# Attention with its exponentials' buffers placed ahead by how long each is needed, and a first unit that lends two steps

## The chip, the cores and the metric

The kernel runs on one core of one Trainium2 chip. The metric is the device time of one launch in microseconds (us), as the median of several runs. The core has five engines that run side by side, each through its own queue in order: TensorE (PE in the profile; PEld is its weight load), VectorE (DVE), ScalarE (ACT), GpSimd (POOL) and SyncE (SP, which here only issues transfers). They are tied together by semaphores.

## The reference

Two layers are computed on an input of 4 images with 256 channels of 48 x 48 pixels, all in float32. The first layer, cut to what matters here:

```python
x = relu(batch_norm(conv3x3(group_norm(x))))
qkv = einsum('oc,bchw->bohw', qkv_w, x) + qkv_b          # 8 heads of d = 32
attn = softmax(einsum('bhdn,bhdm->bhnm', q, k) * scale)  # N = 48 * 48 = 2304
out = einsum('bhem,bhnm->bhen', v, attn)
x = x + proj_w @ out + proj_b
```

The second layer makes per-pixel filters from a convolution, applies them at five dilations, mixes the six results with a 1 x 1 convolution, and normalises over the batch. The change is in the attention of the first layer alone.

## The kernel before

The four images are taken one after the other. For each, a stage that is bound by TensorE (convolution and the q, k, v products of this image, woven with the dynamic filters of the image before) is followed by an attention stage, which runs without the other. There are therefore four attention stages.

Attention of one image is cut into nine units. Units 0 to 7 are one group of four heads (of the two groups) with 512 queries; unit 8, the last, takes the 256 queries left over for both groups. Each unit walks over the 2304 keys in 18 steps of 128 keys (`NT`), so a stage has 162 steps. The order is written out by hand in the loop at the end of `attention`, as a software pipeline of one step:

- `scores` (step i): TensorE multiplies the keys with the queries, 4 heads, one into a PSUM bank of its own (`so`) and three into another tile (`se`). Then ScalarE takes two exponentials of it, L1339 for one head (128 x 512) and L1340 for three (128 x 1536), into an SBUF tile `p` of 128 x 4 x 512. In the kernel before, all `p` are tiles of one tag with four buffers, used in rotation: step i takes the place of step i - 4, and has to wait until whoever reads that one is done.
- `weigh` (step i - 1, after the scores of step i have been issued): TensorE multiplies `p` with the values into `num` (L1365), and VectorE adds `p` into `acc` (L1380), from which the softmax's denominator is made later. Step 0 has no add of its own: the add of step 1 takes `p` of steps 0 and 1 together, so the place of step 0 is held until then.

In some steps VectorE is spared three quarters of that add: in the steps of `LENT` = 2, 5, 8, 11, 14 of units 1 to 8 (the last unit leaves out 14), VectorE adds only the first head, and GpSimd issues a transfer that adds the three others of `p` into a tile `extra` by itself (L1384, an accumulating transfer; the first of a unit is a plain copy, L1382). Such a step is called lent. The place of a lent `p` is free only when its transfer has landed. Each transfer waits for the one before it, as all write `extra`. At the end of units 1 to 7, VectorE adds `extra` to `acc` (L1387, called the closing add here); the last unit adds it on TensorE. `extra` lies in the first 1536 columns of `ring`, a tile that in the other stages holds convolution weights.

At step 1 of a unit `close(u - 2)` makes the denominators of the unit two back on TensorE (`den`) and divides on VectorE. At the end of a unit ScalarE copies `num` to `ao` (L1390). At step 6 of some units (3, 5, 7, and 8) the attention of finished rows is projected on TensorE and added to the residual on VectorE (L1463, with statistics, L661), and ScalarE does a few pieces of the next image's normalisation (L2562).

Of the kernel before, what the change touches and what calls it, by code (L numbers as in the profile page):

```python
# [8 lines left out]
F32 = mybir.dt.float32  # L9
# [8 lines left out]
P = 128  # L18
# [7 lines left out]
NT = N // P  # L26
# [7 lines left out]
QC = 512  # L34
SAFE = 60.0
LENT = (2, 5, 8, 11, 14)
NEVER = float("inf")
LATE = (4, 3)
AHEAD = 2500.0
# [18 lines left out]
def conv_preact_kernel(  # L58
# [493 lines left out]
    with tc.tile_pool(name="w", bufs=1) as wpool, tc.tile_pool(  # L552
        name="act", bufs=1
# [750 lines left out]
        def attention(b, q, k_, vT, pools, spare, project, scratch, following):  # L1304


            ps_s, ps_a, work0 = pools
            ao = keep("h", f"ao_{b}")
            zeros = work0.tile([P, D], F32, tag="zeros", name=f"zeros_{b}", bufs=1)
            nc.gpsimd.memset(zeros, 0.0)  # L1310

            extra = scratch.rearrange("p (j n) -> p j n", j=3)
            scratch = work0.tile([P, QC], F32, tag="rt", name=f"rt_{b}", bufs=1)

            whole, rest = N // QC * QC, N % QC
            units = [[(g, q0, QC, 0)] for q0 in range(0, whole, QC) for g in range(NH)]
            units.append([(g, whole, rest, g * rest) for g in range(NH)])
            assert NH * rest == QC
            heads = [slice(j * D, (j + 1) * D) for j in range(4)]

            def three(name):
                return ps_s.tile([P, 3, 512], F32, tag="s", name=name)

            def scores(u, m):
                s1, s3 = ps_a.tile([P, 512], F32, tag="one", name=f"so_{b}_{u}_{m}"), three(f"se_{b}_{u}_{m}")
                for g, q0, n, at in units[u]:
                    for j, r in enumerate(heads):
                        dst = s3[:, j - 1] if j else s1  # L1330
                        nc.tensor.matmul(  # L1331
                            dst[:, at : at + n],
                            k_[r, g, m * P : (m + 1) * P],
                            q[r, g, q0 : q0 + n],
                            start=True,
                            stop=True,
                        )
                p = work0.tile([P, 4, QC], F32, tag="p", name=f"p_{b}_{u}_{m}", bufs=4)
                nc.scalar.activation(p[:, 0, :], s1, AF.Exp, scale=QS)  # L1339
                nc.scalar.activation(p[:, 1:, :], s3, AF.Exp, scale=QS)  # L1340
                return p

            state = {}
            last = len(units) - 1

            def weigh(u, m, p):
                if m == 0:
                    state[u] = dict(
                        num=ps_a.tile([P, 512], F32, tag="num", name=f"num_{b}_{u}"),
                        acc=work0.tile([P, 4, QC], F32, tag="acc", name=f"acc_{b}_{u}"),  # L1350
                    )
                st = state[u]
                several, end = len(units[u]) > 1, u == last
                if end and m >= NT - 2:
                    sums(u, p, m == NT - 2, m == NT - 1)
                    if m == NT - 2:
                        sums(u, st["acc"], False, False)
                        sums(u, extra, False, False, 1)
                if several and m == 0:

                    for j, r in enumerate(heads):
                        nc.tensor.matmul(st["num"][r, :], zeros, p[:, j, :], start=True, stop=False)
                for i, (g, q0, n, at) in enumerate(units[u]):
                    for j, r in enumerate(heads):
                        nc.tensor.matmul(  # L1365
                            st["num"][r, at : at + n],
                            vT[:, m, g * P + j * D : g * P + (j + 1) * D],
                            p[:, j, at : at + n],
                            start=(m == 0 and not several),
                            stop=(m == NT - 1 and i == len(units[u]) - 1),  # L1370
                        )
                if end and m >= NT - 2:
                    return
                if m == 0:
                    st["first"] = p
                else:
                    other = st["first"] if m == 1 else st["acc"]
                    lend = u > 0 and m in LENT[: len(LENT) - end]
                    js = slice(0, 1 if lend else 4)
                    nc.vector.tensor_tensor(st["acc"][:, js], other[:, js], p[:, js], ALU.add)  # L1380
                    if lend and m == LENT[0]:
                        nc.gpsimd.dma_start(out=extra, in_=p[:, 1:])  # L1382
                    elif lend:
                        nc.gpsimd.dma_start(out=extra, in_=p[:, 1:], accum_op=ALU.add)  # L1384
                if u and m == NT - 1 and not end:
                    rest = st["acc"][:, 1:]
                    nc.vector.tensor_tensor(rest, rest, extra, ALU.add)  # L1387
                if m == NT - 1 and not end:
                    g, q0, n, _ = units[u][0]
                    nc.scalar.copy(ao[:, g, q0 : q0 + n], st["num"])  # L1390

            def sums(u, rhs, start, stop, first=0):
                if start:
                    state[u]["den"] = three(f"den_{b}_{u}")[:, 0, :]
                for j, r in enumerate(heads[first:]):
                    nc.tensor.matmul(
                        state[u]["den"][r, :], ones, rhs[:, j, :], start=start, stop=stop
                    )

            def close(u):  # L1400

                if u < last:
                    sums(u, state[u]["acc"], True, True)
                else:
                    busy(ps_a.tile([P, 512], F32, tag="one", name="warm"), 5)
                st = state.pop(u)
                t = scratch
                nc.vector.transpose(t, st["den"])
                rc = work0.tile([P, QC // D], F32, tag="rc", name=f"rc_{b}_{u}")
                nc.vector.reciprocal(rc, t.rearrange("p (k d) -> p k d", d=D)[:, :, 0])  # L1410
                nc.vector.transpose(
                    t.rearrange("p (k d) -> p k d", d=D),
                    rc.unsqueeze(2).to_broadcast([P, QC // D, D]),
                )
                for g, q0, n, at in units[u]:
                    dst = ao[:, g, q0 : q0 + n]
                    src = dst if u < last else st["num"][:, at : at + n]
                    nc.vector.tensor_tensor(dst, src, t[:, at : at + n], ALU.mult)

            steps = [(u, m) for u in range(len(units)) for m in range(NT)]  # L1420
            prev = None
            chunk = 0
            for i, (u, m) in enumerate(steps):
                ps = scores(u, m)


                if m == 1 and u > 1:
                    close(u - 2)
                if prev is not None:
                    weigh(*steps[i - 1], prev)  # L1430
                prev = ps
                if m == 2 and u == last:
                    close(u - 1)
                if m == 6 and (u % NH == 1 or u == last):
                    while (chunk + 1) * CH <= units[u if u == last else u - 1][0][1]:
                        pp = three(f"pp_{b}_{chunk}")
                        pp = [pp[:, o] for o in range(NH)]
                        if spare:
                            spare.pop(0)()
                        project(chunk, ao, pp)  # L1440
                        chunk += 1
            assert not spare
            weigh(*steps[-1], prev)
            following[0]()
            close(last)
            following[1]()
            return ao, chunk
# [918 lines left out]
        for b in range(B + 1):  # L2366

            with tc.tile_pool(name=f"work1_{b}", bufs=2) as work1, tc.tile_pool(
                name=f"ps_c_{b}", bufs=2, space=PSUM
            ) as ps_c, tc.tile_pool(  # L2370
                name=f"ps_w_{b}", bufs=1 + (b == B), space=PSUM
            ) as ps_w, tc.tile_pool(
                name=f"ps_k_{b}", bufs=3 if b == B else 2, space=PSUM
            ) as ps_k, tc.tile_pool(
                name=f"ps_y_{b}", bufs=1, space=PSUM
# [194 lines left out]
            with tc.tile_pool(name=f"work0_{b}", bufs=2) as work0, tc.tile_pool(  # L2570
                name=f"ps_s_{b}", bufs=2, space=PSUM
# [3 lines left out]
                    lambda c, ao, pp, b=b, n=norm1: project(b, c, ao, pp, n), scratch, following,  # L2575
# [76 lines left out]
```

## Time and profile before

| | |
|---|---|
| runs shown | 2721.27, 2724.35, 2724.39 us; median 2724.35 us |
| profiled execution: time | 2722.09 us |
| profiled execution: span from first to last instruction | 2720.2 us |
| mean granted TensorE clock | 0.989 of full speed |
| attention stage of images 0 to 3 begins about | 152, 808, 1470, 2109 us |
| busy in 152 to 518 us (image 0): VectorE, ScalarE, GpSimd | 324.35, 323.22, 32.10 us of 366 |
| full add L1380 (128 x 2048), median | 2292 ns |
| add of a lent step (128 x 512), least | 682 ns |
| closing add L1387 (128 x 1536), 28 of them | 1757 ns |
| exponentials L1339 and L1340, mean | 599 and 1449 ns |
| transfers issued on GpSimd: L1382 (32), L1384 (124) | 555 and 849 ns to issue |

The durations are of one profiled execution, the runs are separate ones. In a row of the profile `acc<-acc,p` means that the instruction writes `acc` and reads `acc` and `p`; `se` and `so` are the scores, and `ring<-p` are the transfers of lent steps, since `extra` is a piece of `ring`. "Idle before" is the time for which the engine stood still ahead of an instruction, and the name after the arrow is what ended it. Where an instruction waited for several semaphores, the one that came last is named. TensorE's busy time is modelled from pipelined matmuls, so its share is not a measure of how much room it has.

### The profile page before, as it was taken

To read this page: it belongs to the slowest core of one execution; us is meant where nothing else is said; L and a number is where in the kernel's file an instruction comes from. 1 tells how busy PE (TensorE), PEld (TensorE's weight loads), DVE (VectorE), ACT (ScalarE), POOL (GpSimd) and SP (SyncE) were. 2 spreads that over 40 slices of the span, in tenths; PEclk is the share of its full clock that TensorE was granted. 3 is DMA by queue.
4 is the path that set the end of the run, shared out by engine and by line. 5 is a ranking of instruction groups with operands and counts; after the bars stand their busy time and mean duration, and the time that the engine had idled before them with its cause. 6 is when DMAs were issued, how large, how long until landed. Compare 5 with 4: busy or idle time off the path is not lost. (4 is left out here: it accounts for less than half of the span.)

```text
span 2720.2 us, 42536 instructions
## 1 busy us (share of the span) xinstructions
PE 2607.0 (96%) x16938; PEld 1102.1 (41%) x16938; DVE 2082.2 (77%) x2029; ACT 1806.3 (66%) x2287; POOL 809.3 (30%) x885
## 2 busy tenths in 40 slices
PE   6999999999999999999999999999989999999996
PEld 5632222555562222355555222245546222235554
DVE  7768888757739898857774988885775888885676
ACT  4479888734449898854445888884444888875344
POOL 5200100477520010067750000007775000100453
PEclk9999999999999999999999999999999999999998
DMA  4805445323252445423324354452324444432456
GB/s 174 223 13 105 108 98 110 90 60 108 65 104 58 99 95 108 99 74 87 94 63 84 76 105 99 94 111 75 84 73 120 107 100 99 99 88 72 121 165 219
DMA packets 136942, 273.67 MB, mean 101 GB/s; under 512 B 58024, under 2 KB 98384, under 8 KB 135712
## 3 DMA queue, kind: packets, MB, share of 16 engines
q0 software_dynamic: 26256, 137.71, 22.1%
q1 hardware_dynamic: 110480, 133.17, 18.3%
q8 instruction: 135, 2.21, 0.3%
q14 instruction: 71, 0.58, 0.1%
HBM read 112.12 MB, written 36.04 MB: 54 GB/s over the span
## 5 line engine op out<-in xcount | busy, mean ns | idle before, releaser
L1380 DVE TENSOR_TENSOR acc<-acc,p 128x2048 f32<-128x2048 f32 (+1 forms) x568 | 1052.0, 1852 | 121.0 <-ACT p L1340 71.6
L1340 ACT ACTIVATE p<-se 128x1536 f32<-128x1536 f32 x648 | 938.7, 1449 | 0.0
L1331 PE MATMUL so<-q,k 32*128 32x512 f32 (+1 forms) x1440 | 729.1, 594 | 18.5 <-ACT p L1339 15.9
L1331 PE MATMUL se<-q,k 32*128 32x512 f32 (+1 forms) x4320 | 737.8, 594 | 0.0
L1365 PE MATMUL num<-p,vT 128*32 128x512 f32 (+1 forms) x5760 | 711.9, 561 | 2.2 <-ACT ao L1390 2.2
L1339 ACT ACTIVATE p<-so 128x512 f32<-128x512 f32 x648 | 388.4, 599 | 195.2 <-PE se L1331 89.0
L1331 PEld LDWEIGHTS so<-q,k 32*128 32x128 f32 x1440 | 216.7, 183 | 535.6 <-ACT p L1339 492.0
L1834 POOL TENSOR_TENSOR near<-near,prod 128x384 f32<-128x384 f32 x352 | 353.3, 1037 | 255.3 <-DVE prod L1828 246.4
L1384 POOL DMA_DIRECT2D ring<-p x124 | 105.5, 851 | 776.4 <-ACT p L1340 481.4
L1365 PEld LDWEIGHTS num<-p,vT 128*32 128x32 f32 x5760 | 137.1, 108 | 480.2 <-issue 449.7
L1828 DVE TENSOR_TENSOR prod<-wb,pad 128x768 f32<-128x768 f32 x192 | 181.9, 953 | 84.6 <-ACT wb L1815 51.8
L1331 PEld LDWEIGHTS se<-q,k 32*128 32x128 f32 x4320 | 227.3, 183 | 5.1 <-ACT p L1340 4.1
L1815 ACT COPY wb<-ws 128x384 f32<-128x384 f32 x216 | 108.5, 506 | 166.0 <-DVE prod L1828 129.0
L1382 POOL DMA_DIRECT2D ring<-p x32 | 17.9, 559 | 632.2 <-ACT p L1340 485.1
L1992 PE MATMUL py<-far,wsc 128*128 128x384 f32 x512 | 169.9, 487 | 0.0
L1536 PE MATMUL pg<-pad,wcat 128*45 128x384 f32 x864 | 146.7, 490 | 8.5 <-ACT lg L1594 8.5
L1255 PE MATMUL pq<-hid,wqkv 128*128 128x384 f32 x384 | 133.1, 501 | 15.0 <-ACT hid L1125 12.8
L1504 ACT COPY far<-far 128x512 f32<-128x512 f32 x86 | 90.2, 1108 | 81.1 <-PE far L1762 77.8
L1992 PEld LDWEIGHTS py<-far,wsc 128*128 128x128 f32 x512 | 96.2, 190 | 66.0 <-issue 1.8
L1255 PEld LDWEIGHTS pq<-hid,wqkv 128*128 128x128 f32 x384 | 73.1, 194 | 69.2 <-ACT hid L1125 15.1
L1380 DVE TENSOR_TENSOR acc<-p,p 128x2048 f32<-128x2048 f32 x36 | 82.2, 2285 | 20.8 <-ACT p L1340 14.6
L1736 DVE COPY_PREDICATED amat<-along_y,bmat 128x768 f32<-128x768 uint32 x72 | 92.0, 1277 | 2.4
(334 smaller groups left out, 2865.1 us busy)
## 6 DMA issues: line engine op xcount, KB each, us to landing
ring<-p POOLq DMA_DIRECT2D x156, 768.0 KB, 5.7
ws<-w_d SPq DMA_DIRECT2D x216, 192.0 KB
ring<-u_d SPq DMA_DIRECT2D x36, 512.0 KB
pad<-in_x SPq DMA_DIRECT2D x14, 1152.0 KB
xst<-in_x POOLq DMA_DIRECT2D x36, 192.0 KB, 3.7
x_d<-pad SPq DMA_DIRECT2D x36, 192.0 KB
u_d<-pad SPq DMA_DIRECT2D x12, 512.0 KB
y_d<-y SPq DMA_DIRECT2D x13, 384.0 KB
```

Source lines behind the costliest of these rows:

```text
L1255: nc.tensor.matmul(pq[:, :CH], wqkv[:, i, s, g * P : (g + 1) * P], hid[:, i, cols], start=(i == 0), stop=(i == NH - 1),)
L1331: nc.tensor.matmul(dst[:, at : at + n], k_[r, g, m * P : (m + 1) * P], q[r, g, q0 : q0 + n], start=True, stop=True,)
L1339: nc.scalar.activation(p[:, 0, :], s1, AF.Exp, scale=QS)
L1340: nc.scalar.activation(p[:, 1:, :], s3, AF.Exp, scale=QS)
L1365: nc.tensor.matmul(st["num"][r, at : at + n], vT[:, m, g * P + j * D : g * P + (j + 1) * D], p[:, j, at : at + n], start=(m == 0 and not s ...
L1380: nc.vector.tensor_tensor(st["acc"][:, js], other[:, js], p[:, js], ALU.add)
L1384: nc.gpsimd.dma_start(out=extra, in_=p[:, 1:], accum_op=ALU.add)
L1536: nc.tensor.matmul(pg[64 * s : 64 * s + NG, :CH], wcat[:, ii, k, :], shifted(ii, cc, k // 3 - 1, k % 3 - 1), start=(i == 0 and k == 0), st ...
L1815: nc.scalar.copy(pw[:, :CH], fetched[c, k][0])
L1828: nc.vector.tensor_tensor(prod.rearrange("p h (r w) -> p h r w", w=WW), wb, src, ALU.mult)
L1834: nc.gpsimd.tensor_tensor(cat[:, h], cat[:, h], prod[:, h], ALU.add)
L1992: nc.tensor.matmul(py[c][:, o, :CH], wsc[:, n * NH + i, o * P : (o + 1) * P], rhs, start=(n == 0 and i == 0), stop=(n == order[-1] and i = ...
```

## The change

It has two parts. First, which of the four places a `p` gets is no longer a rotation but is worked out ahead for all 162 steps: each of four places has a due time; a step takes the place that is due first (the lowest number among equals), and sets its due time five steps on where the step is lent, three steps on otherwise. Each place becomes a tag of its own with one buffer. The engines still wait for the actual readers of the place; the due times only choose which place. Second, unit 0 lends too, in steps 9 and 14 (`FIRST`), and so does a closing add. A function `lends` now says which steps of a unit are lent; for units 1 to 8 these are the same as before.

```diff
+FIRST = (9, 14)
...
+            last = len(units) - 1
+            steps = [(u, m) for u in range(len(units)) for m in range(NT)]
+
+            def lends(u):
+                return FIRST if not u else LENT[:-1] if u == last else LENT
+
+            until, home = [0] * 4, {}
+            for i, (u, m) in enumerate(steps):
+                home[u, m] = until.index(min(until))
+                until[home[u, m]] = i + (5 if m in lends(u) else 3)
...
-                p = work0.tile([P, 4, QC], F32, tag="p", name=f"p_{b}_{u}_{m}", bufs=4)
+                p = work0.tile(
+                    [P, 4, QC], F32, tag=f"p{home[u, m]}", name=f"p_{b}_{u}_{m}", bufs=1
+                )
...
-                    lend = u > 0 and m in LENT[: len(LENT) - end]
+                    lend = m in lends(u)
                     js = slice(0, 1 if lend else 4)
                     nc.vector.tensor_tensor(st["acc"][:, js], other[:, js], p[:, js], ALU.add)
-                    if lend and m == LENT[0]:
+                    if lend and m == lends(u)[0]:
                         nc.gpsimd.dma_start(out=extra, in_=p[:, 1:])
                     elif lend:
                         nc.gpsimd.dma_start(out=extra, in_=p[:, 1:], accum_op=ALU.add)
-                if u and m == NT - 1 and not end:
+                if m == NT - 1 and not end:
                     rest = st["acc"][:, 1:]
                     nc.vector.tensor_tensor(rest, rest, extra, ALU.add)
```

More of the change, by code (lines that the diff above doesn't have):

```diff
@@ L1343, in attention @@
             state = {}
-            last = len(units) - 1
             def weigh(u, m, p):
@@ L1418, in close @@
                     nc.vector.tensor_tensor(dst, src, t[:, at : at + n], ALU.mult)
-            steps = [(u, m) for u in range(len(units)) for m in range(NT)]
             prev = None
```

## The prediction, made before the changed kernel was run

> **What bounds the kernel now.** I read the page first, then the row of waits of the first exponential's line, then the timelines of ScalarE, GpSimd and VectorE around a few waits.
>
> The page (busy us, share, count; for groups: busy, mean ns of one, idle time before it):
>
> ```profile
> PE 2607.0 (96%) x16938; PEld 1102.1 (41%) x16938; DVE 2082.2 (77%) x2029; ACT 1806.3 (66%) x2287; POOL 809.3 (30%) x885
> ...
> L1380 DVE TENSOR_TENSOR acc<-acc,p 128x2048 f32<-128x2048 f32 (+1 forms) x568 | 1052.0, 1852 | 121.0 <-ACT p L1340 71.6
> L1340 ACT ACTIVATE p<-se 128x1536 f32<-128x1536 f32 x648 | 938.7, 1449 | 0.0
> ...
> L1339 ACT ACTIVATE p<-so 128x512 f32<-128x512 f32 x648 | 388.4, 599 | 195.2 <-PE se L1331 89.0
> ```
>
> TensorE's 96% says little here, as matmuls overlap. What counts is the attention stage: four images, each 366 to 371 us, 162 steps of two exponentials. In undisturbed steps the starts of the first exponential lie 2.067 us apart and ScalarE has no gap at all, so ScalarE sets the pace there. Any idle time before L1339 then lengthens the kernel. What that idle time waited for (view of line L1339):
>
> ```profile
> its engine sat idle before it (us, times) until:
>   PE se L1331: 89.0, 163
>   PE so L1331: 25.1, 31
>   DMA ring<-p: 23.9, 25
>   DVE acc L1380: 10.9, 22
>   issue: 2.5, 1
>   PE num L1365: 1.2, 1
> ```
>
> The TensorE rows are mostly the projections (step 6 to 7 of some units) and the denominators (steps 1 to 3), which this change leaves alone. The next rows are the subject: a place of `p` still being read by the accumulating transfer or by VectorE. One such case, timelines of ScalarE and GpSimd (start, duration, idle before it):
>
> ```profile
> 219.82 0.60 ACT L1339 ACTIVATE p<-so 128x512 f32<-128x512 f32 x1
> 220.31 1.45 ACT L1340 ACTIVATE p<-se 128x1536 f32<-128x1536 f32 x1
> 222.27 0.60 ACT L1339 ACTIVATE p<-so 128x512 f32<-128x512 f32 x1 [0.51 <-DMA ring<-p]
> ...
> 226.41 0.60 ACT L1339 ACTIVATE p<-so 128x512 f32<-128x512 f32 x1 [0.37 <-PE se L1331]
> ```
> ```profile
> 209.63 0.86 POOL L1384 DMA_DIRECT2D ring<-p  x1 [5.43 <-ACT p L1340]
> 215.88 0.85 POOL L1384 DMA_DIRECT2D ring<-p  x1 [5.38 <-ACT p L1340]
> 222.70 0.85 POOL L1384 DMA_DIRECT2D ring<-p  x1 [5.97 <-DMA ring<-p]
> ```
>
> This is unit 1, step 15 of the first image. Its place was lent at step 11, the transfer went out at 215.88 and landed about 6.3 us later, and the exponential starts the moment it lands. The next transfer, at 222.70, waited for the same landing. The line view of L1384 gives the spread of landings:
>
> ```profile
> DMA to landing us min/median/max: 5.7/5.8/7.4
> ```
>
> With four places in rotation a lent place comes round three whole steps after its exponentials end: 3 x 2.067 = 6.2 us. Issue (0.3 us later) plus landing (5.7 or more) is 6.0 or more, so the rotation has 0.1 to 0.4 us to spare, and any landing over 5.9 makes ScalarE wait. Last, VectorE where unit 0 passes into unit 1:
>
> ```profile
> 187.35 9.48 DVE L1380 TENSOR_TENSOR acc<-acc,p 128x2048 f32<-128x2048 f32 x4
> 196.74 2.29 DVE L1380 TENSOR_TENSOR acc<-p,p 128x2048 f32<-128x2048 f32 x1
> 199.13 11.87 DVE L1380 TENSOR_TENSOR acc<-acc,p 128x512 f32<-128x512 f32 x7
> ```
>
> A full add takes 2.29 and follows the last by 2.39, against a step of 2.067, so unit 0, which lends nothing, falls 0.33 us further behind with each of its 17 adds, until the places run out: ScalarE's timeline shows waits of 0.46, 0.46 and 0.27 for VectorE from 194.52 on.
>
> **What the Trainium skill says.** "DMA: Bandwidth & Descriptors", section "Rules for kernel authors": an accumulating DMA must wait for an earlier one's semaphore before it touches the same bytes. The trace agrees: L1384 waited 266.1 us in 45 cases for the landing before it, so transfers form a chain. "Perfetto Trace Analysis", section "Optimization Strategy": repeated gaps on the engine that should be saturated can mean too few buffers. The row of 25 waits for `ring<-p` is that. "SBUF — State Buffer", section "Who interferes with whom", says a DMA never contends with a compute engine; the full add takes 2.28 to 2.29 us with and without a transfer in flight here, so I charge none.
>
> **The change part by part.**
>
> *Places by due time.* I followed the new rule by hand. In units 2 to 7 a lent place returns after six steps (after five for step 5), steps 0, 1, 7 and 17 keep four, and nine others (3, 4, 6, 9, 10, 12, 13, 15, 16) get three. Per image 3 such shortened places are in unit 0, 8 in unit 1, 9 in each of 2 to 7, 7 in unit 8: 72, or 288 in all.
>
> What it removes: from ScalarE's timeline I took every start of L1339 less the one before, less 2.067. Summed over units 1 to 8 and steps 8 to 17 and 0 (where lent places return, and the echo: a wait of TensorE's of +0.25 two steps later and -0.24 between), the excess is 5.6, 9.1, 10.1 and 7.4 us in the four images, 32.1 together. Not all goes. Units without a place wait still show 0.05, the last unit 0.24: 28 x 0.05 + 4 x 0.24 = 2.4. Some 1.6 at 1668 is a spot where TensorE itself ran slow (eight matmuls took 2.20 instead of 1.07). That leaves 28.1.
>
> Does a lent place then wait at five steps? It is free for 4 x 2.067 = 8.3 us. The slowest step-5 case of the trace was issued 0.3 after its exponentials and landed 7.3 later: 7.6. At six steps it is 10.3; the worst chain (image 2, unit 4: landings 6.03, 5.73, 7.08, 5.74, each next issue 0.53 after a landing) recomputed without ScalarE's pauses has its latest landing 7.9 after the exponentials. No wait; bounds 0 and 3 us.
>
> Do three steps suffice? The place is wanted 2 x 2.067 = 4.1 us after its exponentials. Step by step I compared the end of the add with the start of the exponential three steps on: spare time is 1.0 to 2.2 us in plain units and 0.67 at step 6 where a projection runs (its two updates and statistics stand before that add on VectorE). A wait that does bind shows 0.10 of that as signal time, so 0.57 is truly spare. I take 0; upper bound 5 us. Behind a waiting exponential would stand all of ScalarE, then TensorE's next scores.
>
> *Unit 0 lends steps 9 and 14.* Two adds go from 2.29 to 0.68, 1.61 less each; VectorE gains the closing add of `extra`, 1.76 as in row L1387. In unit 0 the add of step 10 ended 0.7 to 1.2 us after the exponential of step 13 began, those of 15 and 16 2.3 after theirs: with three-step places and no lending they would bind. With 1.6 off at step 10 it is 0.4 to 0.9 early, with 3.2 off 15 and 16 are 0.9 and 0.2 to 0.6 early: tight but free. Into unit 1 VectorE carries 3.2 - 1.86 (add and gap) = 1.3 us less lag than now, enough to end the waits there. Their size: steps 1 to 6 of unit 1 hold 4.5 us of excess over the four images; the copy of `ao` on ScalarE, which stays, costs 0.33 in the first of these steps, 1.3 in all. 3.2 goes, plus 0.2 in unit 0 itself. The transfer (0.53 and 0.85 us on an idle GpSimd) falls in a stretch with the DMA engines empty (share 0.00 at 170 to 190). The four closing adds, 7.0 us in all, are hidden behind the exponentials; uncovered, that would be the price. `extra` lies in the first half of `ring`; the block loaded there ahead of the stage goes into its last third, so nothing waits on it. Unit 1's first lend (step 2) must now follow unit 0's closing add; that ends about 6.2 us after step 17's exponentials, the lend is due at 6.7.
>
> Sum: 28.1 + 3.2 + 0.2 = 31.5 off the stage. What follows starts from its end, so all of it counts. The profiled execution took 2722.1 (span 2720.2); less 31.5 is 2690.6. The median of the runs lies 2.3 above that execution; between the two I say 2692. Late next: TensorE's projections and denominators, and ScalarE's own 2.067.
>
> **The rivals.**
>
> *Half of it returns as waits on the chain of transfers.* Landing plus reissue is 5.75 + 0.53 = 6.28 against a lending period of 6.20, so without ScalarE's pauses the chain slips by 0.08 a transfer, and by up to 1.5 at each crowded one. If two crowded ones often met in one unit, perhaps half of the 28 would remain: 2706. Against it: never more than two over 6.3 in one unit.
>
> *No difference.* The places were not the cause: for instance the granted clock (mean 0.989, and the slow spot at 1668) falls as TensorE's pauses vanish: 2722. 1% of clock in a stage that ScalarE paces costs little, which speaks against it.
>
> *Slower: the three-step places wait for VectorE.* One mechanism: the release of a place by its add reaches ScalarE later than the spare 0.67 to 2.2. It decides from about 1.5 us of extra delay; at 1.75 the 288 places would wait some 0.15 each on average, 43 us: 2735 (an estimate). For it: VectorE has only 0.7 to 1 us of idle per three steps of a lending unit. Against it: units with no pause at all exist in the trace (unit 3 of image 0) and keep those margins.
>
> **How the numbers follow.** Forecast 0.79 (own range 2686 to 2699), half 0.09, no difference 0.05, slower 0.07. The range runs from 2685 (a run-to-run spread of 3 and no residue) to 2706, up to the half. A difference under 0.2%, 5.4 us, cannot be told from none: faster 0.88, same 0.05, slower 0.07.
>
> **What would show it.** In the row of L1339, `DMA ring<-p` and `DVE acc` nearly gone, TensorE rows 89.0 and 25.1 smaller only by the echoes; the stage 358 to 363 us an image; transfers 156 to 164 at unchanged landing times; closing adds 28 to 32. A new sizeable `DVE acc` row with starts at steps 9 or 13 would show the three-step places wrong; lasting `DMA ring<-p` at step 10 the five-step ones.

## The result, and the profile after

The changed kernel takes 2690.34 us (median of 4 runs, 2688.22 to 2694.2) against 2722.81 us (2718.02 to 2724.39) for the kernel before in the same measurement. The ratio is 0.9878, with a 95% interval of 0.9864 to 0.9892: some 33 us less. The profiled execution has a span of 2687.6 us against 2720.2. Lines have moved by 10 or 11: the two exponentials are now L1350 and L1351, the add of `p` is L1390, the closing add L1397, the transfers L1392 (first of a unit) and L1394.

What the first exponential waited for, in the changed kernel (us, times):

```profile
its engine sat idle before it (us, times) until:
  PE se L1340: 62.7, 61
  PE so L1340: 25.1, 31
  issue: 3.2, 1
```

The rows for `ring<-p`, for VectorE's `acc` and for `num` are gone: no exponential of the 648 waits for its place any more. The row of `se` fell from 89.0 us in 163 cases to 62.7 in 61. Some 17 us of what fell away is the echo: a start that a place held up is followed by a small wait for TensorE two steps later. Another 7.2 us in 37 cases were place waits under TensorE's name. In the kernel before, those exponentials began 0.10 us after the landing of the transfer from their place, just as the 25 cases of the row `DMA ring<-p` did, and 7 of the 22 under VectorE's name as well. So landings held up more exponentials than that row names. `so` stayed at 25.1: mostly the denominators, which the change does not touch.

The transfers themselves did not become faster (line view of L1394; the second fence gives the landing times):

```profile
its engine sat idle before it (us, times) until:
  ACT p L1351: 545.2, 83
  DMA ring<-p: 140.8, 24
```
```profile
DMA to landing us min/median/max: 5.7/5.8/7.7
```

The row `DMA ring<-p` has 24 cases here and had 45 before, but this does not mean that fewer transfers wait for the one before: the landing is often hidden behind ScalarE's name. By the landing times, 75 of the 128 accumulating transfers start 0.53 or 0.54 us after the landing of the one before, and in the kernel before it was 70 of 124 (0.53 to 0.58 us). The transfers still form a chain, then, and land in 5.7 to 7.7 us (5.7 to 7.4 before); only no exponential waits for them any more. Where unit 0 passes into unit 1, VectorE's and ScalarE's timelines of the first image now read:

```profile
185.46 10.28 DVE L1390 TENSOR_TENSOR acc<-acc,p 128x2048 f32<-128x2048 f32 x5
195.77 1.76 DVE L1397 TENSOR_TENSOR acc<-acc,ring 128x1536 f32<-128x1536 f32 x1
197.45 2.29 DVE L1390 TENSOR_TENSOR acc<-p,p 128x2048 f32<-128x2048 f32 x1
```
```profile
194.04 0.63 ACT L1350 ACTIVATE p<-so 128x512 f32<-128x512 f32 x1
194.53 1.48 ACT L1351 ACTIVATE p<-se 128x1536 f32<-128x1536 f32 x1
196.38 0.60 ACT L1350 ACTIVATE p<-so 128x512 f32<-128x512 f32 x1 [0.36 <-PE se L1340]
196.87 1.45 ACT L1351 ACTIVATE p<-se 128x1536 f32<-128x1536 f32 x1
198.44 0.60 ACT L1350 ACTIVATE p<-so 128x512 f32<-128x512 f32 x1
```

The closing add at 195.77 is new work, and yet the add of steps 0 and 1 (197.45 to 199.74) ends before step 4's exponential wants the place of step 0 at 200.51. The waits of 0.46, 0.46 and 0.27 us for VectorE have given way to one of 0.36 for TensorE.

Where the 32.6 us of span came from, from the starts of the first exponential, four images summed. "Excess" is what the distance from one start to the next has over 2.067 us:

| us | before | after | less |
|---|---|---|---|
| the four attention stages | 1477.1 | 1442.7 | 34.4 |
| of it: excess at steps 8 to 17 and 0 of units 1 to 8 | 32.1 | 1.1 | 31.0 |
| of it: excess at steps 1 to 6 of unit 1 | 4.5 | 2.0 | 2.5 |
| of it: excess at steps 8 to 17 of unit 0 | 0.3 | 0.1 | 0.2 |
| of it: a wait for TensorE at step 2 of unit 0 of the last image | 1.8 | 1.1 | 0.7 |
| everything else | 1243.1 | 1244.9 | -1.8 |

The last row is made of +2.1 ahead of the first stage, +1.4, +0.1 and -1.9 between the stages, and nothing after the last. The first stage begins at 154.5 us in this execution, at 152.4 in that of before, and between 152.2 and 153.7 in those of the experiments, so executions differ by about this much. Two pieces of the gain in the stages are such differences too. The 0.7 us at the start of the last image, and 1.6 of the 31.0 us, come from short stretches in which TensorE ran at half its clock; they fell differently in the two executions (see the last section).

### The profile page after: what moved, and what is told of

It is laid out like the page before. It is cut to its first block, busy times and chain, and to the rows that moved or that the text cites. A ratio compares the mean times of both kernels' runs of the same rounds, so it can differ in the third digit from the quotient of the medians.

```text
span 2687.6 us, 42540 instructions
## 1 busy us (share of the span) xinstructions
PE 2590.6 (96%) x16938; PEld 1095.0 (41%) x16938; DVE 2075.3 (77%) x2033; ACT 1808.6 (67%) x2287; POOL 814.3 (30%) x893
## 5 line engine op out<-in xcount | busy, mean ns | idle before, releaser
L1390 DVE TENSOR_TENSOR acc<-acc,p 128x2048 f32<-128x2048 f32 (+1 forms) x568 | 1039.3, 1830 | 96.2 <-ACT p L1351 44.5
L1351 ACT ACTIVATE p<-se 128x1536 f32<-128x1536 f32 x648 | 938.1, 1448 | 0.0
L1375 PE MATMUL num<-p,vT 128*32 128x512 f32 (+1 forms) x5760 | 699.5, 561 | 1.7 <-ACT ao L1400 1.7
L1350 ACT ACTIVATE p<-so 128x512 f32<-128x512 f32 x648 | 388.4, 599 | 158.9 <-PE se L1340 62.7
L1394 POOL DMA_DIRECT2D ring<-p x128 | 109.1, 852 | 809.3 <-ACT p L1351 545.2
L1375 PEld LDWEIGHTS num<-p,vT 128*32 128x32 f32 x5760 | 129.1, 108 | 475.0 <-issue 448.4
L1392 POOL DMA_DIRECT2D ring<-p x36 | 20.1, 558 | 560.6 <-ACT p L1351 272.1
L1390 DVE TENSOR_TENSOR acc<-p,p 128x2048 f32<-128x2048 f32 x36 | 82.3, 2285 | 21.5 <-ACT p L1351 14.6
```

What stands on the lines that cost most here:

```text
L1375: nc.tensor.matmul(st["num"][r, at : at + n], vT[:, m, g * P + j * D : g * P + (j + 1) * D], p[:, j, at : at + n], start=(m == 0 and not s ...
```

## The experiments

**The two parts, each alone, and a control.** The edits are to the changed kernel.

Places by due time only; unit 0 lends nothing:

```diff
-                return FIRST if not u else LENT[:-1] if u == last else LENT
+                return () if not u else LENT[:-1] if u == last else LENT
...
-                if m == NT - 1 and not end:
+                if u and m == NT - 1 and not end:
                     rest = st["acc"][:, 1:]
```

> The due-time places without the first unit's lending (unit 0 lends nothing and has no closing add; its places then rotate by four as before). Theory: the waits of the first exponential for lent places were the main cost, worth 28 us, so 2723 - 28 = about 2695 (2692 to 2699), with no 'DMA ring<-p' row before the first exponential and the 'DVE acc' row left only at the start of unit 1, about 1 to 1.3 us an image. Rival (the gain came mainly from VectorE's lag out of unit 0): about 2718.

2693.88 us, ratio 0.9901 (0.9887 to 0.9915). ScalarE's timeline at the same spot as above (image 0, from step 2 of unit 1):

```profile
194.36 0.60 ACT L1350 ACTIVATE p<-so 128x512 f32<-128x512 f32 x1 [0.46 <-DVE acc L1390]
194.85 1.45 ACT L1351 ACTIVATE p<-se 128x1536 f32<-128x1536 f32 x1
196.75 0.60 ACT L1350 ACTIVATE p<-so 128x512 f32<-128x512 f32 x1 [0.46 <-DVE acc L1390]
...
198.95 0.60 ACT L1350 ACTIVATE p<-so 128x512 f32<-128x512 f32 x1 [0.26 <-DVE acc L1390]
```

These are the waits of the kernel before, to 0.01 us. All place waits of the kernel are here: the row of waits before the first exponential has no `ring<-p` and this for VectorE:

```profile
  DVE acc L1390: 5.5, 14
```

So the due times removed the waits for transfers by themselves (the excess at steps 8 to 17 and 0 is 1.8 us, from 32.1), and left the lag out of unit 0 alone.

Unit 0 lends, but places rotate by four:

```diff
-                home[u, m] = until.index(min(until))
+                home[u, m] = i % 4
```

> Unit 0 lends steps 9 and 14, but all places rotate by four. Theory: only the start of unit 1 gains, 3.4 us: about 2719.5 (2717 to 2722); the 'DMA ring<-p' waits stay at 20 us or more. Rival (first unit is the main thing): 2700 or less.

2718.29 us, ratio 0.9981 (0.9974 to 0.9988). The excess at steps 1 to 6 of unit 1 is 2.0 us, as in the changed kernel; that at steps 8 to 17 and 0 is 29.5. The waits, from the same view:

```profile
  PE se L1340: 86.4, 158
  PE so L1340: 25.1, 31
  DMA ring<-p: 23.6, 26
  DVE acc L1390: 4.4, 6
```

The six left under `acc` stand at steps 12 and 15, where the places of lent steps come back, and not at the start of unit 1.

Four tags, but rotation and no lending in unit 0 (both edits above together):

> A control: four tags of one buffer each instead of one tag of four buffers, but places in rotation and no lending in unit 0. Theory: the tags do nothing by themselves, so 2723 within 4 us, and the same waits as before. Rival (the way the buffers are tagged changes which semaphores are waited for, and that is the gain): 2705 or less.

2724.42 us, ratio 1.0003 (0.9995 to 1.0011), with 25.9 us in 26 waits for `ring<-p`. The tags by themselves make no difference that can be measured. The parts add up: 0.9901 and 0.9981 multiply to 0.9882, beside 0.9878 for both.

**How much room the places have.** Lent places kept for seven steps, which squeezes others:

```diff
-                until[home[u, m]] = i + (5 if m in lends(u) else 3)
+                until[home[u, m]] = i + (7 if m in lends(u) else 3)
```

> The changed kernel with seven steps in place of five for lent places. Worked out by hand, steps 6 (units 1 to 8) and 9 (units 2 to 8) then get their place taken back after two steps. Theory: an add ends 2.3 us after the exponentials and later, the place is wanted at 2.2; so steps 6 and 9 wait 0.2 to 0.5 each in plain units, and where a projection runs (add of step 6 late) about 1.5 more. About 10 us an image, 40 in all: 2728 (2710 to 2740), with a 'DVE acc' row of 30 to 45 us. Rival (VectorE's adds do not decide over places, only landings do): 2690.

2721.97 us, ratio 0.9994 (0.9984 to 1.0004): the whole gain is gone, and no transfer is waited for. VectorE is waited for instead:

```profile
  PE se L1340: 75.5, 98
  DVE acc L1390: 38.5, 37
  PE so L1340: 25.1, 31
```

Timelines of VectorE and ScalarE in image 1, unit 3, where the place of step 6 is wanted at step 8:

```profile
947.09 0.56 DVE L662 BATCH_NORM_STATS2 stn<-pad 128x6 f32<-128x384 f32 x1
947.57 4.67 DVE L1390 TENSOR_TENSOR acc<-acc,p 128x2048 f32<-128x2048 f32 x2
```
```profile
946.38 0.60 ACT L1350 ACTIVATE p<-so 128x512 f32<-128x512 f32 x1 [1.12 <-PE se L1340]
946.87 1.44 ACT L1351 ACTIVATE p<-se 128x1536 f32<-128x1536 f32 x1
949.94 0.60 ACT L1350 ACTIVATE p<-so 128x512 f32<-128x512 f32 x1 [1.63 <-DVE acc L1390]
```

The first of the two adds is that of step 6. It starts when the projection's statistics are done and ends about 949.86, 2.29 us later; the exponential follows at 949.94. The size was right (30 to 45 us expected in that row), the list was not complete: besides step 8 (late by 0.22 to 0.5 in plain units, by 1.5 where a projection runs), step 3 of unit 1 was late by 1.3 to 1.5, since the place of step 0 there returned after three steps instead of four. One of the 37 waits stands in unit 0 of image 2. The places of step 9, also taken back after two steps, have no wait of their own: the add of step 9 ends 0.09 to 0.13 us before the exponential of step 11, as close as where a place does bind (0.09 to 0.10), after the echo had put off step 10 by 0.22 to 0.25. Three steps are thus too few for step 0, and two for step 6.

VectorE held up at step 6 where a projection runs, the spot whose room the prediction had read:

```diff
+                    if m == 6 and u in (3, 5, 7):
+                        for j in range(2):
+                            nc.vector.tensor_reduce(spent[:, j : j + 1], p[:, j], AX.X, ALU.max)
                     nc.vector.tensor_tensor(st["acc"][:, js], other[:, js], p[:, js], ALU.add)
```

> The changed kernel with two useless reductions of p (128 x 512 each, about 0.7 us) on VectorE ahead of the add of step 6 in units 3, 5 and 7 (12 places in all), to measure how much room the three-step places have where a projection runs. Theory: 0.57 us of room, so 1.4 - 0.57 = about 0.8 us of waiting at step 9 in each of the 12, 10 us in all: about 2700, the waits named 'DVE acc'. Rival (there is more room than that, since places are released earlier or VectorE catches up): 2690 to 2692 and no such row.

2695.99 us, ratio 0.9881 (0.9859 to 0.9902), which does not differ clearly from the changed kernel's 0.9878; the median is 4 us below the 2700 expected. The trace does tell them apart. Image 1, unit 3, VectorE and ScalarE:

```profile
938.93 1.26 DVE L1393 TENSOR_REDUCE spent<-p 128x1 f32<-128x512 f32 x2
940.11 5.47 DVE L1394 TENSOR_TENSOR acc<-acc,p 128x2048 f32<-128x2048 f32 x3
```
```profile
939.81 0.60 ACT L1351 ACTIVATE p<-so 128x512 f32<-128x512 f32 x1
940.30 1.44 ACT L1352 ACTIVATE p<-se 128x1536 f32<-128x1536 f32 x1
942.49 0.60 ACT L1351 ACTIVATE p<-so 128x512 f32<-128x512 f32 x1 [0.74 <-DVE acc L1394]
```

The reductions put the add off by 940.11 - 938.93 = 1.18 us, and the exponential of step 9 comes 942.49 - 939.81 - 2.067 = 0.61 us late. The room was therefore 1.18 - 0.61 = 0.57 us. There are 12 such waits (8.9 us of idle time in all, 7.3 us of excess), one for each of the 12 edited places and none elsewhere.

This is not the least room in the changed kernel. From the end of an add to the exponential that takes its place there are 0.66 to 0.69 us at step 6 with a projection, but 0.28 at step 16 of unit 0 in image 2 (0.64 to 0.79 in the other images), and 0.37 at step 0 of units 2 to 7, although that place keeps four steps.

**What holds the rest.** Denominators of a unit at step 3 of the next one, rather than at step 1 of the one after:

```diff
-                if m == 1 and u > 1:
-                    close(u - 2)
+                if m == 3 and u:
+                    close(u - 1)
...
-                if m == 2 and u == last:
-                    close(u - 1)
```

> The changed kernel, with the denominators of a unit made one unit later at step 3 instead of two units later at step 1. Asks what holds the 1.33 us that steps 1 to 3 of units 2 to 7 still lose. Theory: it is TensorE's work for the denominators plus ScalarE's copy of the outputs, two separate costs that stay wherever they stand: 2690 within 4 us, with the excess moved from steps 2 and 3 to 4 and 5. Rival: VectorE, which is late at that point (its add of step 1 ends only 0.4 us before its place is wanted), holds TensorE through the denominators' PSUM tile; then the move wins up to 0.5 us a unit, about 2676.

2695.47 us, ratio 0.9906 (0.9891 to 0.9921). ScalarE in image 1, unit 2, step 2 and then steps 4 and 5:

```profile
888.07 0.60 ACT L1350 ACTIVATE p<-so 128x512 f32<-128x512 f32 x1 [0.36 <-PE se L1340]
...
893.07 0.60 ACT L1350 ACTIVATE p<-so 128x512 f32<-128x512 f32 x1 [1.00 <-PE so L1340]
...
895.34 0.60 ACT L1350 ACTIVATE p<-so 128x512 f32<-128x512 f32 x1 [0.33 <-PE se L1340]
```

Less 2.067, the steps are late by 0.22 and 0.27 (steps 1 and 2: the copy of the outputs on ScalarE) and by 0.87 and 0.21 (steps 4 and 5: the denominators on TensorE). Apart they cost 1.57 us a unit; together, at steps 1 to 3 of the changed kernel, 1.33. The excess moved as the theory said, but the median lies 1.5 us above the expected range, and the four stages take 1453.1 us, 10.4 more than in the changed kernel. That the move costs 0.24 in each of units 2 to 7 was not expected; apparently part of one wait hides in the other when they meet, which was not tried further. Unit 1, which had no denominators to make before, now has 1.07 more in each image. A late VectorE is not what holds these steps: here it had itself been idle for 0.90 us before it took up the denominators, until TensorE had made them.

```profile
891.19 0.72 DVE L1418 STREAM_TRANSPOSE rt<-den 128x512 f32<-128x512 f32 x1 [0.90 <-PE den L1406]
```

An attempt at a faster version: the edit above, and the copy on VectorE ahead of the add of step 17:

```diff
+                    if m == NT - 1 and not end:
+                        g, q0, n, _ = units[u][0]
+                        nc.vector.tensor_copy(ao[:, g, q0 : q0 + n], st["num"])
                     other = st["first"] if m == 1 else st["acc"]
...
-                    nc.scalar.copy(ao[:, g, q0 : q0 + n], st["num"])
```

> An attempt at a faster version: the copy of the outputs at a unit's end goes from ScalarE to VectorE, ahead of the add of step 17, and the denominators are made at step 3 of the next unit (as in e7), so that VectorE has room at the unit's start. In e7 the copy costs 0.49 us at steps 1 and 2 of every unit after the first. Theory: that goes, less what TensorE waits for the later copy: 32 x 0.4 = 13 us below e7, about 2682 (2678 to 2688). Rival: TensorE's first value matmul of the next unit waits for the copy on the busier VectorE, and the gain is lost: 2695 or more.

2687.78 us, ratio 0.9858 (0.9841 to 0.9874). The interval overlaps that of the changed kernel, and the four stages sum to 1441.9 us against 1442.7: no clear gain over it. The copy's 0.49 us did go from steps 1 and 2. But in units 2, 4 and 6 step 7 now waits for VectorE, for the place of step 4, whose add comes after the denominators' work (image 1, unit 2):

```profile
897.83 0.60 ACT L1350 ACTIVATE p<-so 128x512 f32<-128x512 f32 x1 [0.38 <-DVE acc L1393]
```

With its echo that is 0.25 us a unit. Against the run with the later denominators alone the stages are 11.3 us shorter, near the 13 expected, so moving the copy did what it should; most of this only makes good the 10.4 us that the later denominators cost. The expected 2682 was 6 us too low.

## Why the prediction was right

The median is 2690.34 us where 2692 was forecast, and the forecast's mechanism holds at each step.

*ScalarE sets the pace, and its idle time ahead of the first exponential lengthens the kernel.* The stages lost 34.4 us and the span 32.6. The work between and after the stages did not give it back: the distances differ by -1.9 to +2.1 us, to either side. Of the 34.4, some 32 are owed to the change and 2.3 to where the half-clock stretches fell, beside a forecast of 31.5.

*Place waits for lent steps, put at 28.1 us.* They measured 31.0. The mechanism is shown by the two parts alone. One term was mis-sized: I had left 2.4 us as a residue of steps without a place wait, and 1.1 remain. The 0.05 a unit that I read as permanent fell to 0.02 or 0.03, the last unit's 0.24 to 0.10. The other difference is luck: I had taken off 1.6 for a spot where TensorE ran slow, and no such spot fell into these steps of the changed kernel's execution. The control with four tags, which has none there either, loses 2.40 us in that unit (image 2, unit 4) where the kernel before lost 3.92; but its excess over all units is 31.6, so the landings alone make executions differ by about 1 us.

*The start of unit 1, put at 3.2 us.* It measured 2.5. The copy of `ao` costs 0.22 and 0.27 us at two steps, and I had counted 0.33 at one. In the places-only kernel, which lacks this part, the excess at unit 1 is exactly that of the kernel before.

*Three steps suffice.* Yes, with the room that was read from the trace: 0.57 us where a projection runs, both as read and as measured by holding up the add. The tightest place, step 16 of unit 0, held with 0.28 us between add and exponential, where 0.2 to 0.6 had been worked out. The rival that ends slower was real as a mechanism and wrong in size: with one step less for a few places of each unit (lent places kept for seven steps) the whole gain is lost.

*No wait at five and six steps for lent places.* None came, but with less room than the prediction had it. I recomputed the worst chain to a landing 7.9 us after the exponentials. In the changed kernel, image 0, unit 6, GpSimd's and ScalarE's timelines show a later one:

```profile
403.23 0.85 POOL L1394 DMA_DIRECT2D ring<-p  x1 [6.09 <-ACT p L1351]
411.44 0.85 POOL L1394 DMA_DIRECT2D ring<-p  x1 [7.36 <-ACT p L1351]
417.74 0.85 POOL L1394 DMA_DIRECT2D ring<-p  x1 [5.44 <-ACT p L1351]
```
```profile
423.76 0.60 ACT L1350 ACTIVATE p<-so 128x512 f32<-128x512 f32 x1
424.25 1.45 ACT L1351 ACTIVATE p<-se 128x1536 f32<-128x1536 f32 x1
425.83 0.60 ACT L1350 ACTIVATE p<-so 128x512 f32<-128x512 f32 x1
```

The transfer at 403.23 took 7.7 us to land, so the next two went out late, the second (step 11) 2.4 us after its exponentials; it landed 6.38 us on, at 424.1, which is 8.8 us after them. Five steps would have given the place back at 423.76, before the landing. It was given back at 425.83, at six steps, as the prediction had worked out for it, with 1.7 us to spare. Of the places that do return after five, the tightest is step 5 of the same unit: its transfer landed 7.97 us after its exponentials (7.6 had been taken as the worst), 0.43 us before the place was wanted. By the starts of this execution, five steps everywhere would have been too short for two places, steps 11 and 14 of this unit, by 0.36 and 0.18 us; such a kernel was not run.

*The rival with waits on the chain of transfers.* Its mechanism is there: three in five transfers start on the landing of the one before, and at most 3.1 us after their exponentials (0.29 where nothing is ahead). Five and six steps take this up, so none of it reaches ScalarE.

*The rival of the granted clock.* The mean is 0.989 in both profiled executions, so the gain was not lost to it.

*The closing adds and transfers of unit 0 cost nothing.* Four closing adds and eight transfers more, and no exponential after them waits for VectorE; the first stage ends 5.9 us sooner after it begins (360.2 us instead of 366.1).

## What to carry to other kernels

When buffers rotate and their contents live unequally long, look for waits whose release comes just after the rotation's turn: here 6.0 us and more of life against 6.2 us of turn. If most of the tiles are free long before theirs, choosing places by due time buys room for the long-lived ones without more memory. Before doing so, read the spare time of the short-lived ones from the trace, step by step, because it is that which is spent: asking seven steps instead of five for the lent places gave all 33 us back. And look for waits on a landing by the landing times, not by the name in the row alone, since a landing can stand under another engine's name.

## What the runs showed of the hardware that had not been expected

In the profiled execution of the kernel before, at 1664 to 1668 us, TensorE ran a few matmul groups at about half speed (eight value matmuls in 2.20 us, otherwise 1.07; a scores matmul in 1.22, otherwise 0.69) and cost ScalarE about 1.6 us. The granted TensorE clock was low in just this stretch. From the view of stretches of the kernel before (from and to; length; busy us of TensorE, its weight load, VectorE, ScalarE and GpSimd; granted clock, DMA share, GB/s):

```profile
1660.00:1664.00 4.00, 2.18 (x24) 0.48 (x16) 1.69 (x2) 1.72 (x3) 0.85 (x1) 1.00 0.15 29
1664.00:1668.00 4.00, 4.00 (x24) 0.85 (x16) 3.23 (x2) 2.47 (x3) 0.00 (x0) 0.58 0.97 194
1668.00:1672.00 4.00, 4.00 (x36) 0.95 (x32) 2.94 (x2) 3.44 (x4) 0.00 (x0) 0.99 0.02 3
```

Such a stretch lies at the start of the last image's attention too, in both kernels: the granted clock was 0.50 at 2109 to 2114 us in the kernel before and at 2084 to 2088 in the changed one, and eight value matmuls took 1.94 us in either. This is the wait at step 2 of unit 0 in the table; it is 1.8 us in one and 1.1 in the other. The places-only execution has none in its stages. What brings these stretches about was not tried.

Two short delays at neighbouring steps, one on ScalarE and one on TensorE, cost less together (1.33 us) than apart (0.49 + 1.08 us).
